# Two-layer attention block in float32 on one core: the deviation of a normalisation as a power on GpSimd, and two places in the order of the work

## The chip, the core and the metric

The kernel runs on one core of one Trainium2 chip. The metric is the device time of one execution in microseconds. One more execution was recorded by the hardware profiler; its own time stands beside its span (first to last instruction) in the table below, and every duration in this document is from such a recorded execution. Names of engines in the profile: PE is TensorE (PEld its weight loads), DVE is VectorE, ACT is ScalarE, POOL is GpSimd, SP is SyncE, which here only issues DMAs.

## The reference, cut to what matters

The input is a map of 2 x 512 channels x 64 x 32, so 2 batches of 2048 tokens with 512 channels, all in float32. Two layers follow each other:

```python
x = conv_attention(x)              # 8 heads of 64, softmax over 2048 tokens, output product, bias, + x
t = tokens(x)
t = t + landmark_attention(ln(t))  # 256 landmarks, pseudo-inverse by 6 iterations, 33-tap convolution of v
t = t + ffn(ln(t))                 # two 512 x 512 products, one of them dequantised from 4 bit
def ln(v, eps=1e-5):               # over the 512 channels
    m = mean(v, -1); s = var(v, -1)
    return (v - m) / sqrt(s + eps)
```

The change concerns the factor 1 / sqrt(s + eps) of both uses of `ln`, and the place of some steps around it and around the landmark attention.

## The kernel before, in words

Channels lie on the 128 partitions (KC = 4 chunks), tokens along the free axis in blocks of TB = 512, so a batch has NTB = 4 blocks. Heads go in pairs (NPAIR = 4). The program is written in the order in which each engine is to do its work: that order is kept on TensorE, VectorE, ScalarE and GpSimd, and units of work are interleaved by hand with Python generators. `advance(gens, n)` takes the next n units of the generators in a list and returns how many it got; where the list is empty it returns 0.

The stages, in order of time:

1. Layer 0 (to about 1420 us of the profile). `attention0` walks over pairs of a batch; each step makes scores (`sc_f`, L1072), an Exp on ScalarE (`p_f`, L1080), a running sum of exponentials on VectorE (`acc_f`, L1090) and products with the values (`av_f`, L1102). Beside it run fillers: the projections of the next pair, and, in the first pairs of batch 1, `finish0_units` for batch 0: output product and residual (`yp_f` L968, `xr_f` L975), store of x1, and the first normalisation, `norm0_steps`, which stores the normalised xh.
2. The same finish for batch 1, interleaved with the projections of layer 1 (about 1380 to 1520 us): the loop over t with `norm0(t)`, `out0(t)` and `more`, which holds the projections (`pp` L1245), landmarks (`L` L1250), and small products (`pr` L1313) of the other pairs.
3. Layer 1, pair after pair (to about 2640 us). `pinv` does the iterations of the pseudo-inverse on the matrices M and R, with `chunk(c)` and `last(i)` called between to do the attention of the pair before (`attn1_...`) and the pair after (`attn3_...`). From the fifth pair on also `finish1_units` of batch 1.
4. The last four blocks of batch 0 (to the end): output product, second normalisation, and `fp_g`, the product with the merged feed-forward matrix.

`statistics` makes the mean of a block with a product with `mean_w` (every partition then holds it, `mean_n` or `mean_g`, L990), subtracts it (`xn`, L991), squares on ScalarE (L994, L997), sums the squares on VectorE (L1002, L1003), takes their mean on TensorE (`var_n` or `var_g`, L1006), and then the square root on ScalarE with eps as bias (L1008). The result `rstd` is a tile of 128 x 512.

`norm0_steps` (layer 0's end; `rstd_n`) then takes the reciprocal on VectorE (L1023) and multiplies: half of xn on GpSimd (L1025), half on VectorE (L1026); GpSimd issues the store of xh (L1027). In batch 0 there is one xn buffer, so the next block waits for that store. `Finish1.steps` (second normalisation; `rstd_g`) takes the reciprocal on VectorE (L1660); xn stays undivided, and the factor is applied after the product: y = fp * rstd (L1683), added to the residual (L1684) and stored. Each of the two is done for 8 blocks, so there are 16 such deviations.

Exp and square root are in different activation tables on ScalarE, so loads of tables (ACT_TABLE_LOAD) stand around the square roots.

In `chunk(c)`, `attn1_sums` sums the exponentials of the pair before with ones (`rs`, L779) and copies them (L1619), `attn1_inverse` takes the reciprocal (L1624) and spreads it with eight DMAs on SP (L790), and `attn1_end`, in the next chunk, multiplies (L1631) and adds into o on GpSimd (L1632).

Of the kernel before, what the change touches and what calls it, by code (L numbers as in the profile page):

```python
# [10 lines left out]
F32 = mybir.dt.float32  # L11
I32 = mybir.dt.int32
AF = mybir.ActivationFunctionType
ALU = mybir.AluOpType
# [649 lines left out]
def fast_path(  # L664
# [96 lines left out]
    nc.vector.memset(mean_w, 1.0 / C)  # L761
    ones = const.tile([P, D], F32, name="ones1")
    nc.vector.memset(ones, 1.0)
    eps = const.tile([P, 1], F32, name="eps1")
    nc.vector.memset(eps, 1e-5)
    b0_sb = const.tile([P, KC], F32, name="b0_f")
# [26 lines left out]
    def advance(gens, n=1):  # L793


        made, i = 0, 0
        while made < n and i < len(gens):
            got = next(gens[i], gens)
            if got is gens:
                gens.pop(i)  # L800
            elif got is GAP:
                i += 1
            else:
                made += 1
        return made
# [177 lines left out]
    def statistics(xb, xn, part, name, squares, row, apart=False):  # L983


        nc.vector.tensor_tensor(part, xb[:, :2, :], xb[:, 2:, :], ALU.add)
        nc.vector.tensor_tensor(part[:, 0, :], part[:, 0, :], part[:, 1, :], ALU.add)
        yield
        mean = bank(f"mean_{name}")
        nc.tensor.matmul(mean, lhsT=mean_w, rhs=part[:, 0, :], start=True, stop=True)  # L990
        nc.vector.tensor_tensor(xn, xb, mean.unsqueeze(1).to_broadcast([P, KC, TB]), ALU.subtract)  # L991
        yield
        sq, *others = squares()
        nc.scalar.activation(sq, xn[:, :2, :], AF.Square)  # L994
        n = 2 // len(others)
        for i, other in enumerate(others):
            nc.scalar.activation(other, xn[:, 2 + i * n : 2 + (i + 1) * n, :], AF.Square)  # L997
        if apart:
            yield
        for i, other in enumerate(others):  # L1000
            to = sq[:, i * n : (i + 1) * n, :]
            nc.vector.tensor_tensor(to, to, other, ALU.add)  # L1002
        nc.vector.tensor_tensor(sq[:, 0, :], sq[:, 0, :], sq[:, 1, :], ALU.add)  # L1003
        yield
        var = bank(f"var_{name}")
        nc.tensor.matmul(var, lhsT=mean_w, rhs=sq[:, 0, :], start=True, stop=True)  # L1006
        rstd = row()
        nc.scalar.activation(rstd, var, AF.Sqrt, bias=eps, scale=1.0)  # L1008
        yield rstd

    def out0_units(b, t, xb, oTs):
# [4 lines left out]
    def norm0_steps(b, t, xb, xn, part):  # L1016

        toks = slice(t * TB, (t + 1) * TB)
        name = f"n0_{b}_{t}"
        squares = lambda: (xb[:, :2, :], xb[:, 2:, :])  # L1020
        for rstd in statistics(xb, xn, part, name, squares, lambda: deviation(name)):
            yield
        nc.vector.reciprocal(rstd, rstd)  # L1023
        wide = rstd.unsqueeze(1).to_broadcast([P, 2, TB])
        nc.gpsimd.tensor_tensor(xn[:, 2:, :], xn[:, 2:, :], wide, ALU.mult)  # L1025
        nc.vector.tensor_tensor(xn[:, :2, :], xn[:, :2, :], wide, ALU.mult)  # L1026
        nc.gpsimd.dma_start(chunked(xh_d[b])[:, :, toks], xn)  # L1027
        yield
# [605 lines left out]
    class Finish1:  # L1634
# [17 lines left out]
        def steps(self, row, apart=False):  # L1652
            def squares():
                sq = apool.tile([P, 2, TB], F32, tag="acc", name=f"sq_{self.name}")
                return sq, *(row_of(f"sq{k}_{self.name}").unsqueeze(1) for k in (2, 3))

            self.xn = self.xn()
            for rstd in statistics(self.xb, self.xn, self.xn[:, :2, :], self.name, squares, row, apart):
                if rstd is not None:
                    nc.vector.reciprocal(rstd, rstd)  # L1660
                    self.rstd = rstd
                yield

# [156 lines left out]
    for t in range(NTB):  # L1820
        more_out = [out0(t + 1)] if t + 1 < NTB else []
        advance(more)

        next(norm)
        advance(more_out or more)
        if last is not None:
            next(last)
        advance(more_out or more)
        next(norm)
        advance(more_out, 2)  # L1830
        advance(more, 2)

        next(norm)
        last = norm
        while more_out:
            advance(more_out)
        if t + 1 < NTB:
            norm = norm0(t + 1)
            next(norm)
# [90 lines left out]
    for n, pair in enumerate(todo):  # L1930
        before = todo[n - 1] if n else None
        after = todo[n + 1] if n + 1 < len(todo) else None
        if n + 2 < len(todo):
            todo[n + 2].prefetch_w()
        if n == NPAIR + 2:
            before.load_o(kvpool.tile([P, S], F32, tag="k", name=f"o2_{n - 1}"))
        if n == NPAIR + 3:

            xb = as_block(kvpool.tile([P, NST, P], F32, tag="v", name="xb_g_early"))
            xn = lambda: block_of(lpool, "xn", "xn_g_early")  # L1940
            early.append(Finish1(1, NTB - 1, [p.o for p in todo[:NPAIR]], xb, xn, True))
            before.load_o(late_buffer(f"o2_{n - 1}"))
        pair.iteration_start()
        while vals:
            advance(vals)
        if after:
            after.prefetch()
            after.attn3_begin()
        if n + 2 < len(todo):
            vals = [values(n + 2)]  # L1950
        if n:
            q = late_buffer if n > NPAIR + 1 else lambda name: kvpool.tile([P, S], F32, tag="k", name=name)
            pair.prefetch1(q(f"q2_{pair.name}"))

        def chunk(c):
            nonlocal landmarks
            if before and 0 < c <= n_ones:
                before.attn1_end(c - 1)
            if n == NPAIR and c == 1:

                finish.append(finish1_units(1, [p.o for p in todo[:NPAIR]], early))
            advance(finish)
            if c == NTB:
                if after:
                    landmarks = after.landmarks_values()
                    next(landmarks)
                    drain(convolution(n + 1))
                else:
                    advance(finish, 2)
                return  # L1970
            ones_before = before if c < n_ones else None
            if ones_before:
                if c:
                    before.attn1_scores(c, 0)
                    before.attn1_scores(c, 1)
                before.attn1_add(c)
            if after:
                for s, bank_of in ((2 * c, product_bank), (2 * c + 1, bank)):
                    after.attn3_scores(s, bank_of)
                    after.attn3_add(s)  # L1980
            else:
                advance(finish)
            if ones_before:
                before.attn1_values(c)
            if after:
                after.attn3_values(2 * c)
            else:
                advance(finish)
            if ones_before:
                before.attn1_sums(c)  # L1990
            if after:
                after.attn3_values(2 * c + 1)
            if ones_before:
                before.attn1_inverse(c)
            if n == NPAIR + 2 and c % 2:
                advance(finish)

        def last(i):
            nonlocal start
            if i == 1 and after:  # L2000
                next(landmarks)
                drain(landmarks)
                start = after.start_values()
            if i == 2 and after:
                next(start)
            else:
                advance(vals)
            if i == 3 and after:
                next(start)
            if n_ones < NTB:  # L2010

                if i == 0:
                    before.attn1_scores(n_ones, 0)
                    before.attn1_scores(n_ones, 1)
                    before.attn1_add(n_ones)
                if i == 1:
                    before.attn1_values(n_ones)
                if i == 2:
                    before.attn1_sums(n_ones)
                if i == 3:  # L2020
                    before.attn1_inverse(n_ones)
                if i == 5:
                    before.attn1_end(n_ones)
            if i == 5:
                pair.attn1_scores(0, 0)
                pair.attn1_scores(0, 1)
            advance(finish)

        landmarks = start = None
        n_ones = NTB if n + 2 < len(todo) else NTB - 1  # L2030
        pair.pinv(chunk, last)
# [158 lines left out]
```

## Time and profile before

| | |
|---|---|
| median of 2 runs | 2738.23 us (2737.63 to 2738.82) |
| the profiled execution | 2739.02 us, span 2737.2 us, TensorE clock 0.997 |
| TensorE busy | 2695.4 us (98%) |
| VectorE busy | 1631.7 us (60%) |
| ScalarE busy | 906.3 us (33%) |
| GpSimd busy | 162.0 us (6%) |

A group of instructions is given as: line, engine, operation, what it writes and reads with shapes, how many; then busy us and mean ns of one; then the idle time of the engine just before them and what ended it. A line of waits is given as: who waited for what, total us, how often, the longest. In a timeline the first number is the start in us from the span's start, the second the time that the merged entry covers, and the bracket the idle time before it and what ended it. TensorE's matmuls overlap and each float32 matmul leaves two records, so 512 columns take 0.43 us of stream time a record though one is drawn as about 0.6.

### The profile page before, as it was taken

Reading aid. Unit: us, or ns where it says so; the run is one execution under the profiler, and the core shown is the slowest. Engines: PE = TensorE matmul, PEld = TensorE weight load, DVE = VectorE, ACT = ScalarE, POOL = GpSimd, SP = SyncE. Lnnn points to the kernel's source line nnn. Section 1 sums busy time; section 2 is a strip of 40 time slices with the busy share of each in tenths; the row PEclk is TensorE's granted clock in tenths of the full one; section 3 lists DMA queues with packets and bytes.
Section 4 is the critical chain, followed back from the end, with each engine's and each line's share of the span. In section 5 each row is a group of like instructions: output and inputs, shape, how many; then the busy total and the mean of one; then the engine's idle time right before and its main releaser. Section 6 shows DMA issues by size and latency. Waiting matters only on the chain.

```text
span 2737.2 us, 41174 instructions
## 1 busy us (share of the span) xinstructions
PE 2695.4 (98%) x16994; PEld 1361.0 (50%) x16994; DVE 1631.7 (60%) x2087; ACT 906.3 (33%) x1352; POOL 162.0 (6%) x109
## 2 busy tenths in 40 slices
PE   9999999999999999999999999999999999999999
PEld 5343343434443334344344455777677666655344
DVE  3867777664557765656667544445544645465565
ACT  1434444434334334444422223223323223231210
POOL 0101011000001100000002000000000000000000
PEclk9999999999999999999999999999999999999999
DMA  4100000212111200012024632312211112111211
GB/s 147 41 11 24 24 24 24 86 36 70 32 63 57 97 24 20 24 40 77 24 89 163 209 120 93 103 34 87 81 37 62 59 44 87 44 60 53 89 39 47
DMA packets 111476, 173.99 MB, mean 64 GB/s; under 512 B 16176, under 2 KB 67888, under 8 KB 106672
## 3 DMA queue, kind: packets, MB, share of 16 engines
q1 hardware_dynamic: 105136, 150.00, 16.9%
q0 software_dynamic: 5440, 20.97, 2.1%
q8 instruction: 135, 2.21, 0.3%
q14 instruction: 61, 0.50, 0.1%
q10 hardware_dynamic: 704, 0.31, 0.0%
HBM read 90.87 MB, written 63.57 MB: 56 GB/s over the span
## 4 chain that ended last, share of the span: by engine, by line
PE 91%; DVE 5%; DMA 1%; ACT 1%; SPq 1%; issue 1%; POOL 0%; DVEq 0%; ACTq 0%; POOLq 0%
PE sc_f L1072 15%; PE av_f L1102 15%; PE pp L1245 8%; PE pa L1538 5%; PE pb L1538 5%; PE vp_f L953 4%; PE vp L953 4%; PE pp_k_f L905 4%; PE yp_g L968 4%; PE yp_f L968 4%; PE fp_g L1694 4%; PE pp_q_f L905 3%; PE av L1388 2%; PE sc L1367 2%; PE sc L1595 2%; PE av L1611 2%
## 5 line engine op out<-in xcount | busy, mean ns | idle before, releaser
L1090 DVE TENSOR_TENSOR acc_f<-acc_f,p_f 128x1024 f32<-128x1024 f32 x448 | 581.3, 1297 | 209.9 <-ACT p_f L1080 181.4
L1080 ACT ACTIVATE p_f<-sc_f 128x1024 f32<-128x1024 f32 x512 | 496.7, 1022 | 563.9 <-PE sc_f L1072 561.2
L1072 PE MATMUL sc_f<-q_f,k_f 64*64 64x512 f32 x4096 | 491.1, 594 | 2.7 <-ACT p_f L1080 2.7
L1102 PE MATMUL av_f<-p_f,v_f 64*64 64x512 f32 x4096 | 484.3, 589 | 0.0
L1102 PEld LDWEIGHTS av_f<-p_f,v_f 64*64 64x64 f32 x4096 | 156.5, 133 | 283.0 <-issue 283.0
L1072 PEld LDWEIGHTS sc_f<-q_f,k_f 64*64 64x64 f32 x4096 | 145.8, 133 | 285.6 <-issue 261.9
L1245 PE MATMUL pp<-xh,w 128*128 128x512 f32 x512 | 229.5, 600 | 0.7 <-ACT q L1248 0.7
L1538 PE MATMUL pa<-M 128*128 128x192 f32 (+1 forms) x640 | 153.1, 384 | 6.0 <-ACT M L1529 6.0
L1245 PEld LDWEIGHTS pp<-xh,w 128*128 128x128 f32 x512 | 95.3, 191 | 121.3 <-issue 113.8
L1538 PE MATMUL pb<-R 128*128 128x192 f32 (+1 forms) x640 | 149.3, 380 | 0.0
L1538 PEld LDWEIGHTS pa<-M 128*128 128x128 f32 x640 | 109.3, 195 | 27.6 <-ACT M L1529 9.1
L953 PEld LDWEIGHTS vp_f<-wv_f,x 128*128 128x128 f32 x1024 | 115.7, 192 | 13.5 <-issue 11.8
L953 PE MATMUL vp<-w,xh 128*128 128x128 f32 x1024 | 120.9, 276 | 0.0
L953 PEld LDWEIGHTS vp<-w,xh 128*128 128x128 f32 x1024 | 117.0, 192 | 7.2 <-issue 4.6
L905 PE MATMUL pp_k_f<-x,wk_f 128*128 128x512 f32 x256 | 116.0, 606 | 2.8 <-DVE k_f L908 2.4
L953 PE MATMUL vp_f<-wv_f,x 128*128 128x128 f32 x1024 | 118.7, 277 | 0.0
L1538 PEld LDWEIGHTS pb<-R 128*128 128x128 f32 x640 | 106.5, 190 | 23.2 <-DVE M L1551 0.4
L905 PE MATMUL pp_q_f<-x,wq_f 128*128 128x512 f32 x256 | 114.2, 598 | 0.8 <-DVE q_f L908 0.5
L968 PE MATMUL yp_g<-o,wo_f 128*128 128x512 f32 x256 | 114.8, 597 | 0.0
L968 PE MATMUL yp_f<-q_f,wo_f 128*128 128x512 f32 x256 | 113.5, 598 | 0.8 <-DVE xr_f L975 0.8
L1120 POOL TENSOR_TENSOR q_f<-q_f,rinv_f 128x512 f32<-128x512 f32 x32 | 46.7, 1459 | 1039.3 <-DMA rinv_f<-acc_f 761.1
L1551 DVE SCALAR_TENSOR_TENSOR R<-M,pa 128x320 f32<-128x320 f32 (+1 forms) x160 | 59.9, 416 | 67.8 <-PE pa L1538 67.8
(210 smaller groups left out, 2764.8 us busy)
## 6 DMA issues: line engine op xcount, KB each, us to landing
xh<-xh_fd SPq DMA_DIRECT2D x12, 1024.0 KB, 5.5
rinv_f<-acc_f SPq DMA_DIRECT2D x256, 32.0 KB, 1.9
xr_f<-in_x_dram SPq DMA_DIRECT2D x8, 1024.0 KB, 5.2
x_fd<-xr_f POOLq DMA_DIRECT2D x8, 1024.0 KB, 4.8
xh_fd<-xn_f POOLq DMA_DIRECT2D x8, 1024.0 KB, 4.7
k_fd<-k SPq DMA_DIRECT2D x32, 256.0 KB, 2.9
q_fd<-q SPq DMA_DIRECT2D x32, 256.0 KB, 2.9
k<-k_fd SPq DMA_DIRECT2D x8, 1024.0 KB, 6.6
```

The lines of the kernel that those rows point to most:

```text
L905: nc.tensor.matmul(pp, lhsT=w_sb[kind][:, k, cols], rhs=xbs[t][:, k, :], start=k == 0, stop=k == KC - 1)
L953: nc.tensor.matmul(vp[:, j * P : (j + 1) * P], lhsT=xb[:, k, j * P : (j + 1) * P], rhs=w_of(k), start=k == 0, stop=k == KC - 1,)
L968: nc.tensor.matmul(yp, lhsT=wo_sb[:, k, m * P : (m + 1) * P], rhs=oTs[k][:, toks], start=k == 0, stop=k == NPAIR - 1,)
L1072: nc.tensor.matmul(sc[r * D : (r + 1) * D, h, :], lhsT=hd.k[rows, lo : lo + D], rhs=hd.q[rows, t * TB : (t + 1) * TB], start=True, stop=True,)
L1080: nc.scalar.activation(p, sc, AF.Exp, scale=D**-0.5)
L1090: nc.vector.tensor_tensor(acc, first if c == 1 else acc, p, ALU.add)
L1102: nc.tensor.matmul(av[r][half, :], lhsT=hd.v[keys, c, half], rhs=pp[keys, h, :], start=c == 0, stop=c == NST - 1,)
L1245: nc.tensor.matmul(pp, lhsT=self.w[j][:, c, :], rhs=xhs[t][:, c, :], start=c == 0, stop=c == KC - 1)
L1367: nc.tensor.matmul(scs[h][:, j * LM : (j + 1) * LM], lhsT=self.k[rows, c * P : (c + 1) * P], rhs=self.L[0][rows, :], start=True, stop=True,)
L1538: nc.tensor.matmul(dst, lhsT=lhsT[:, k, t * P : (t + 1) * P], rhs=rhs[:, k, :], start=k == 0, stop=k == 1)
L1551: nc.vector.scalar_tensor_tensor(out, m, scale, pr, ALU.mult, ALU.subtract)
L1694: nc.tensor.matmul(fp[:, cols], lhsT=mT[:, k, m * P : (m + 1) * P], rhs=self.xn[:, k, cols], start=k == 0, stop=k == KC - 1,)
```

## The change

The square root becomes an Identity (variance plus eps, out of the accumulator), and GpSimd takes it to the power -0.5 in place, with a constant tile of one column spread over the row. The two reciprocals on VectorE go, and so do 19 of the 20 table loads that lie on the executed path. Two places of the order change. In the loop of stage 2, where no output units are left (the last block), four units of `more` instead of two come between the squares and the variance. In `chunk(c)`, the sums `attn1_sums` come after the second half of `attn3_values` instead of before it.

```diff
@@ constants
     nc.vector.memset(ones, 1.0)
+    power = const.tile([P, 1], F32, name="power1")
+    nc.vector.memset(power, -0.5)
@@ statistics
         nc.tensor.matmul(var, lhsT=mean_w, rhs=sq[:, 0, :], start=True, stop=True)
         rstd = row()
-        nc.scalar.activation(rstd, var, AF.Sqrt, bias=eps, scale=1.0)
+        nc.scalar.activation(rstd, var, AF.Identity, bias=eps, scale=1.0)
+        nc.gpsimd.tensor_tensor(rstd, rstd, power.to_broadcast([P, TB]), ALU.pow)
         yield rstd
@@ norm0_steps
-        nc.vector.reciprocal(rstd, rstd)
         wide = rstd.unsqueeze(1).to_broadcast([P, 2, TB])
         nc.gpsimd.tensor_tensor(xn[:, 2:, :], xn[:, 2:, :], wide, ALU.mult)
         nc.vector.tensor_tensor(xn[:, :2, :], xn[:, :2, :], wide, ALU.mult)
@@ Finish1.steps
                 if rstd is not None:
-                    nc.vector.reciprocal(rstd, rstd)
                     self.rstd = rstd
                 yield
@@ the loop of stage 2
         advance(more_out or more)
         next(norm)
-        advance(more_out, 2)
-        advance(more, 2)
+        advance(more, 2 if advance(more_out, 2) else 4)
 
         next(norm)
@@ chunk(c)
-            if ones_before:
-                before.attn1_sums(c)
             if after:
                 after.attn3_values(2 * c + 1)
             if ones_before:
+                before.attn1_sums(c)
                 before.attn1_inverse(c)
```

In the built order of the engines this moves `var_n` of the last block of batch 1 behind four more `pp` matmuls and two `pr`; it moves `rs` behind four `av` matmuls in 23 chunks; GpSimd gets 16 instructions, each ahead of the product or the addition that follows; VectorE loses 16.

## The prediction

> **What bounds the kernel now.** I read the page's busy times and chain first, then the list of waits by engine, the groups of instructions by shape, and the timeline wherever a statistic of the two normalisations is made. From the page:
>
> ```profile
> PE 2695.4 (98%) x16994; PEld 1361.0 (50%) x16994; DVE 1631.7 (60%) x2087; ACT 906.3 (33%) x1352; POOL 162.0 (6%) x109
> PE 91%; DVE 5%; DMA 1%; ACT 1%; SPq 1%; issue 1%; POOL 0%; DVEq 0%; ACTq 0%; POOLq 0%
> ```
>
> TensorE is the bound: of 2737.2 us it is idle for 41.8. The change takes no matmul away, so it can earn only from those 41.8 us and from matmuls that run slow after an idle stretch. VectorE has time on average, but an in-order VectorE that stands still in the wrong place stops TensorE. The waits of TensorE say where (total, times, longest):
>
> ```profile
> PE pa L1538 <- ACT M L1529: 6.0, 2, 4.6
> PE var_n L1006 <- issue: 3.7, 1, 3.7
> PE wp L1513 <- DVE R L1551: 3.2, 2, 2.1
> PE p_pa L1528 <- DVE M L1502: 2.2, 2, 1.2
> PE mean_n L990 <- DVE xn_f L987: 1.4, 1, 1.4
> PE yp_f L968 <- DVE xr_f L975: 0.8, 1, 0.8
> ```
>
> The work that the change replaces, in groups by shape (busy us, mean ns), with GpSimd's nearest instruction last:
>
> ```profile
> L1023 DVE RECIPROCAL rstd_n<-rstd_n 128x512 f32<-128x512 f32 x8 | 26.7, 3342 | 0.0
> L1660 DVE RECIPROCAL rstd_g<-rstd_g 128x512 f32<-128x512 f32 x8 | 26.8, 3352 | 15.3 <-ACT rstd_g L1008 15.3
> L1008 ACT ACT_TABLE_LOAD x10 | 12.8, 1283 | 7.1 <-PE var_n L1006 7.0
> L1120 POOL TENSOR_TENSOR q_f<-q_f,rinv_f 128x512 f32<-128x512 f32 x32 | 46.7, 1459 | 1039.3 <-DMA rinv_f<-acc_f 761.1 <-DVE acc_f L1090 278.2
> ```
>
> The largest stall that belongs to the change, in the timeline (start, us):
>
> ```profile
> 1486.96 3.34 DVE L1023 RECIPROCAL rstd_n<-rstd_n 128x512 f32<-128x512 f32 x1
> 1489.62 3.70 PE L1245 MATMUL pp<-xh,w 128*128 128x512 f32 x8
> 1494.96 1.21 DVE L1002 TENSOR_TENSOR xr_f<-xr_f 128x1024 f32<-128x1024 f32 x1
> 1496.21 0.69 DVE L1003 TENSOR_TENSOR xr_f<-xr_f 128x512 f32<-128x512 f32 x1
> 1497.00 1.48 PE L1006 MATMUL var_n<-xr_f,mean_w 128*128 128x512 f32 x2 [3.68 <-issue]
> 1498.28 4.95 PE L1245 MATMUL pp<-xh,w 128*128 128x512 f32 x8
> ```
>
> TensorE stands until VectorE ends L1003 at 1496.90. VectorE has no gap there: its reciprocal of the block before (1486.96) is in front. After the stall eight matmul records take 4.95 us where they took 3.70.
>
> **What the Trainium skill says.** "ScalarE: Activation LUTs", What ACT_TABLE_LOAD costs: about 1283 ns for a load and 1380 ns of drain for every switch of set; the same page, Table sets, says identity is filler in every set. The trace agrees on 1283 and shows no drain: the load at 2541.11 starts 0.02 us after the instruction before it. "GPSIMD Engine Reference", Elementwise: bodies of three and more operations go at about 3 a cycle, a two-input add at 2.6 cycles an element. The trace agrees with the second (undisturbed 128x512 products take 1.27 us); neither page nor trace prices a power. "TensorE: Matmul & The Clock Gate", Part 1, has an idle array fall to half clock; the 4.95 against 3.70 above agrees.
>
> **The change part by part.**
>
> *Removed from VectorE:* 16 reciprocals x 3.35 = 53.5 us. *From ScalarE:* 19 of 20 table loads x 1.283 = 24.4 us; the Identity that replaces Sqrt keeps its 0.69. Both are off the path except where a wait above hangs on them:
> - 1497.00: 3.68 idle, + 1.25 slow matmuls, + 0.46 of the longer var = 5.4 us. Twice cured: VectorE is 3.3 us earlier, and the new filler count puts var behind four more pp matmuls and two pr. Next late would be pr, which needs X; VectorE makes X_0 by about 1495, and TensorE reaches pr at about 1496.8.
> - 2449.02: wp waits 1.19 for R, which stands behind the reciprocal L1660 (2445.38 to 2448.73). Gone. The inverse of the row sums behind it starts 4 us earlier, so the DMA for which VectorE idles until 2458.54 lands earlier; that clears 1.00 us at 2461.53.
> - 912.24 (0.82) and 920.80 (1.43): the residual add, and the reuse of the one xn buffer after GpSimd's product and its store, follow the reciprocal of 906.92.
> - 936.26 (0.73): scores wait for an Exp behind the table load at 933.89.
> Sum 10.6 us. The other waits for ScalarE and VectorE (4.6 at 2527, 2.1 at 2440, 1.5 at 2596) have neither a reciprocal nor a load ahead of them and stay.
>
> *Added to GpSimd:* 16 powers of 128x512. Not in the trace. Below: not under a product of the same shape, 1.3 us. Above: a power is a logarithm, a product and an exponential; as polynomials with exponent handling I count 20 to 40 operations for each of 512 elements. At the page's 3 per cycle (1.2 GHz) that is an estimate of 3 to 6 us; if nothing overlaps, at some 4 cycles each, 34 to 68 us. I take **7 us**, near the geometric middle of 1.3 and 40.
>
> It is hidden as long as it ends before its first reader comes up. The room, from the end of Sqrt (less a table load just before it) to that reader's start: batch 0: 17.9, 10.5, 8.4, 7.1 us; batch 1: 11.8, 11.4, 12.5, about 8; first finish: 36.8, 6.6, 4.9, 3.8; last four blocks: 3.9 (the power starts at 2647.9 behind GpSimd's last o add, its reader came at 2651.80), 19.5, 19.5, 3.3. In the finish and the last blocks the reader, y, has 3 to 5 us more, since fp banks stand ready: in the last block VectorE idles 2.0 us twice before 2731.07, so 8.9 us are free; in the block at 2647.9, 6.4, until the squares of the next block are late for var at 2657.89. With 7 us only this one shows: 0.6. Behind a waiting VectorE stand the exponential sums (batch 0), the landmark means and squares (batch 1), R and M of the inverse (finish); TensorE waits for these. GpSimd itself has only o products and x1, xh stores behind it, read much later except for the xn reuse named above.
>
> *Moved:* in 23 chunks rs goes behind the second four av matmuls. The three parts take 0.96 + 0.57 + 1.02 us at 1853.52; sixteen av records in one go take 1.95 at 1763.40, so 0.02 us x 23 = 0.5 is won. But rs, its copy, its reciprocal and the eight spread DMAs on SP start 1 us later. Mostly covered (VectorE idles 0.8 us after that reciprocal at 1857.34), but not at 2515.45, where R follows it at once, nor at 2522.34, where VectorE already waits for that DMA ahead of the 4.6 us stall. I take 1.5 lost: net +1.0 (bounds -0.5 and +3).
>
> Sum: -10.6 + 0.6 + 1.0 = **-9.0 us**. The profiled execution took 2739.0 (span 2737.2 and 1.8 around it), 0.8 over the median, so 2730 against it and **2729** against the median of 2738.2.
>
> **The rivals.**
> 1. *The power is partly exposed* (8 to 18 us). For it: three rooms are under 5 us and no row bounds the power. At 13 us the overruns of all sites add to 64, less some 20 of bank reserve; if half of the rest reaches TensorE, 22 lost against 9 won: about 2752.
> 2. *The power is slow, and VectorE stalls in order behind it* (slower). Place: L1026 and L1683 on VectorE. Price: at 25 us the overruns add to 226, less 20; seven tenths reach TensorE (there is no other work once buffers are full): 144 - 10 gives about 2870. It decides from about 18 us, where the loss passes 54. Against it: GpSimd is 6% busy and its product runs near its price.
> 3. *The cleared waits come back behind others.* GpSimd and VectorE slow each other (products reach 2.3 us beside VectorE work against 1.27), or pr waits for X: half of the gain stays, about 2735.
>
> **How the numbers follow.** Main case 0.54, rival 1 0.20, rival 2 0.16, rival 3 0.10. Two per cent, 55 us, is about what a measurement of this kernel can tell from no change; a gain of that size is more than all 41.8 us of idle time, so faster gets 0.01. Slower is rival 2, 0.16; the rest, 0.83, is within. The range runs from 2722 (power under 4 us, more waits cleared than counted) to 2775 (power of 16 us): the main case, rival 3 and most of rival 1.
>
> **What would show it.** Right: no L1023 and L1660, one table load, powers of 128x512 on GpSimd near 7 us, no idle time before var_n at 1497 and before wp at 2449, TensorE idle near 32 us. Wrong: VectorE idle before L1026 or L1683 released by GpSimd, with TensorE waiting for acc, xn or R just after; a power over 18 us turns the sign beyond doubt. If the power is under 8 us and the time still does not fall, rival 3 holds.

## The result, and the profile after

The changed kernel took 3854.77 us (median of 2 runs, 3854.45 to 3855.09) against 2738.23: a ratio of 1.408 [1.405, 1.410]. It is slower by 1116 us, where the prediction had 2729 and a range of 2722 to 2775. Line numbers of the changed kernel are one to three higher than those of the kernel before. A site is one of the 16 normalisations; the room of a power is the time from its start until its reader is ready for it. Its profiled execution took 3854.45 us, span 3853.0.

From its page: TensorE's busy time, the granted clock in 40 slices, and the chain that ended last.

```profile
PE 2727.2 (71%) x16994; PEld 1377.2 (36%) x16994; DVE 1577.2 (41%) x2072; ACT 880.0 (23%) x1333; POOL 1472.8 (38%) x125
...
PEclk9999999978766999996665999999997968757665
...
PE 56%; POOL 34%; DVE 4%; issue 2%; DMA 1%; SPq 1%; ACT 1%; DVEq 0%; POOLq 0%; ACTq 0%
```

GpSimd rose from 162 us to 1473 and now holds a third of the chain, where it held nothing. TensorE's work is the same 16994 records; its idle time rose from 41.8 to 1125.8, and its busy time by 31.8. These two, 1084.0 and 31.8, are the whole growth of the span, 1115.8. The clock row (tenths of full clock) has its low digits in the stretches of the normalisations and 9s between them.

The two groups of powers (line, engine, operation, shapes, count; busy us, mean ns of one; idle before and what ended it):

```profile
L1011 POOL TENSOR_TENSOR rstd_n<-rstd_n,power 128x512 f32<-128x512 f32 x8 | 655.8, 81976 | 103.8 <-ACT rstd_n L1010 103.8
...
L1011 POOL TENSOR_TENSOR rstd_g<-rstd_g,power 128x512 f32<-128x512 f32 x8 | 655.9, 81984 | 77.8 <-ACT rstd_g L1010 77.8
```

One power of 128x512 takes 82.0 us, not 7. Its readers on VectorE, from the list of waits (who waited for what: total us, times, longest):

```profile
DVE xn_f L1028 <- POOL rstd_n L1011: 598.1, 8, 80.3
DVE y_g L1684 <- POOL rstd_g L1011: 569.0, 8, 81.4
```

All 16 readers stand still, 1167.1 us together, nine tenths of the 1311.7 us of powers. The largest waits of TensorE do not name GpSimd; it waits for what VectorE, or ScalarE beside it, would have done next:

```profile
PE yp_f L970 <- DVE xr_f L977: 337.0, 5, 74.5
PE var_g L1008 <- DVE sq_g L1005: 189.7, 4, 75.2
PE sc L1597 <- DVE y_g L1684: 150.3, 2, 75.4
PE sc_f L1074 <- ACT p_f L1082: 77.5, 9, 75.2
PE tp L1524 <- DVE y_g L1684: 73.2, 1, 73.2
PE pr L1315 <- DVE X L1301: 73.0, 1, 73.0
```

Each longest wait here is one power less 7 to 9 us. The row var_n at 1497, the largest stall that the change was to clear, is gone. One site in the timeline (start, us, then idle time and what ended it in the bracket), the first of batch 0:

```profile
783.72 81.94 POOL L1011 TENSOR_TENSOR rstd_n<-rstd_n,power 128x512 f32<-128x512 f32 x1 [2.35 <-ACT rstd_n L1010]
...
804.46 3.70 PE L970 MATMUL yp_f<-q_f,wo_f 128*128 128x512 f32 x8
808.09 1.95 PE L1074 MATMUL sc_f<-q_f,k_f 64*64 64x512 f32 x16
809.25 1.94 ACT L1082 ACTIVATE p_f<-sc_f 128x1024 f32<-128x1024 f32 x2 [5.29 <-PE sc_f L1074]
809.86 1.90 PE L1104 MATMUL av_f<-p_f,v_f 64*64 64x512 f32 x16
865.70 1.22 DVE L1028 TENSOR_TENSOR xn_f<-xn_f,rstd_n 128x1024 f32<-128x1024 f32 x1 [67.40 <-POOL rstd_n L1011]
866.84 0.74 DVE L977 SCALAR_TENSOR_TENSOR xr_f<-yp_f,b_f,xr_f 128x512 f32<-128x512 f32 x1
867.64 5.39 PE L970 MATMUL yp_f<-q_f,wo_f 128*128 128x512 f32 x8 [55.88 <-DVE xr_f L977]
```

The chain reads from bottom to top. TensorE stands 55.88 us for a bank (a block of the accumulator) that L977 on VectorE must empty; L977 is behind L1028 in VectorE's fixed order; L1028 waits for the power. VectorE stopped at 798.3; TensorE had other work up to 811.8, and then nothing. Eight output-product records right after the stall take 5.39 us; the same eight took 3.70 just before it. While TensorE has nothing to do here, from 812 to 865 us, the granted clock is 0.54 of full. Such slow stretches after a stall make up the additional busy time: the group yp_f alone grew from 113.5 us to 126.1.

### The profile page after: what moved, and what is told of

Read it like the earlier page. It is cut to its first block, busy times and chain, and to the rows that moved or that the text cites. A ratio compares the mean times of both kernels' runs of the same rounds, so it can differ in the third digit from the quotient of the medians.

```text
span 3853.0 us, 41154 instructions
## 1 busy us (share of the span) xinstructions
PE 2727.2 (71%) x16994; PEld 1377.2 (36%) x16994; DVE 1577.2 (41%) x2072; ACT 880.0 (23%) x1333; POOL 1472.8 (38%) x125
## 4 chain that ended last, share of the span: by engine, by line
PE 56%; POOL 34%; DVE 4%; issue 2%; DMA 1%; SPq 1%; ACT 1%; DVEq 0%; POOLq 0%; ACTq 0%
POOL rstd_n L1011 17%; POOL rstd_g L1011 17%; PE sc_f L1074 10%; PE av_f L1104 9%; PE pp L1247 5%; PE pb L1540 3%; PE pa L1540 3%; PE vp L955 3%; PE vp_f L955 3%; PE pp_k_f L907 3%; PE pp_q_f L907 2%; PE yp_g L970 2%; PE yp_f L970 2%; PE sc L1597 2%; DVE acc_f L1092 1%
## 5 line engine op out<-in xcount | busy, mean ns | idle before, releaser
L1011 POOL TENSOR_TENSOR rstd_n<-rstd_n,power 128x512 f32<-128x512 f32 x8 | 655.8, 81976 | 103.8 <-ACT rstd_n L1010 103.8
L1011 POOL TENSOR_TENSOR rstd_g<-rstd_g,power 128x512 f32<-128x512 f32 x8 | 655.9, 81984 | 77.8 <-ACT rstd_g L1010 77.8
L970 PE MATMUL yp_f<-q_f,wo_f 128*128 128x512 f32 x256 | 126.1, 649 | 337.0 <-DVE xr_f L977 337.0
L1634 POOL TENSOR_TENSOR o<-o,rinv 128x512 f32<-128x512 f32 x32 | 44.6, 1395 | 705.3 <-DVE rinv L1633 636.2
L1684 DVE TENSOR_TENSOR y_g<-fp_g,rstd_g 128x512 f32<-128x512 f32 (+1 forms) x33 | 22.0, 666 | 580.2 <-POOL rstd_g L1011 569.0
L1028 DVE TENSOR_TENSOR xn_f<-xn_f,rstd_n 128x1024 f32<-128x1024 f32 x8 | 9.8, 1225 | 598.1 <-POOL rstd_n L1011 598.1
L970 PEld LDWEIGHTS yp_f<-q_f,wo_f 128*128 128x128 f32 x256 | 51.7, 208 | 410.2 <-DVE xr_f L977 341.2
L1597 PE MATMUL sc<-q,L 64*128 64x512 f32 x224 | 62.2, 644 | 151.0 <-DVE y_g L1684 150.3
L1008 PE MATMUL var_g<-sq_g,mean_w 128*128 128x512 f32 x16 | 11.6, 813 | 189.7 <-DVE sq_g L1005 189.7
L1602 ACT ACTIVATE p<-sc 128x512 f32<-128x512 f32 x128 | 66.7, 601 | 250.8 <-PE sc L1597 250.5
```

Source lines behind the costliest of these rows:

```text
L970: nc.tensor.matmul(yp, lhsT=wo_sb[:, k, m * P : (m + 1) * P], rhs=oTs[k][:, toks], start=k == 0, stop=k == NPAIR - 1,)
L1011: nc.gpsimd.tensor_tensor(rstd, rstd, power.to_broadcast([P, TB]), ALU.pow)
L1597: nc.tensor.matmul(sc, lhsT=self.Lk[rows, j * P : (j + 1) * P], rhs=self.q[rows, t * TB : (t + 1) * TB], start=True, stop=True,)
L1602: nc.scalar.activation(p[:, h, :], sc, AF.Exp, scale=D**-0.5)
```

## The experiments

Four questions were open. What does a power cost, and on what does it depend? Does the sum of the prediction hold if the power has the size that was assumed? How much of VectorE's waiting reaches TensorE? And what are the other parts of the change worth without the power?

### The price of a power by itself: e5_price

```diff
 (kernel before, at its start, on constant tiles)
+for p, n in ((P, 512), (P, 128), (P, 32), (P, 4), (1, 128), (16, 128), (32, 128)):
+    nc.gpsimd.tensor_tensor(made[:p, :n], base[:p, :n], power[:p].to_broadcast([p, n]), ALU.pow)
+nc.gpsimd.tensor_tensor(made[:, :128], base[:, :128], power.to_broadcast([P, 128]), ALU.mult)
```

> The kernel before with eight GpSimd instructions on constant tiles at its start: powers of 128x512, 128x128, 128x32, 128x4, 1x128, 16x128 and 32x128 (base 0.7, exponent -0.5) and one product of 128x128. If a power goes column by column[...], time follows the columns alone: 82, 20.5, 5.1, 0.7, and 20.5 us for 1, 16 and 32 partitions. If it goes value by value,[...] 1x128 takes a sixteenth of 16x128, about 1.3 us, while 16, 32 and 128 partitions still take 20.5.

Measured, groups by shape on GpSimd:

```profile
L770 POOL TENSOR_TENSOR bench_out<-bench_in,power 128x512 f32<-128x512 f32 x1 | 82.0, 81982 | 1.3 <-DVE bench_in L767 1.3
L770 POOL TENSOR_TENSOR bench_out<-bench_in,power 128x128 f32<-128x128 f32 x1 | 20.7, 20720 | 0.1
L770 POOL TENSOR_TENSOR bench_out<-bench_in,power 1x128 f32<-1x128 f32 x1 | 20.7, 20715 | 0.1
L770 POOL TENSOR_TENSOR bench_out<-bench_in,power 16x128 f32<-16x128 f32 x1 | 20.7, 20705 | 0.1
L770 POOL TENSOR_TENSOR bench_out<-bench_in,power 128x32 f32<-128x32 f32 x1 | 5.4, 5416 | 0.1
L770 POOL TENSOR_TENSOR bench_out<-bench_in,power 128x4 f32<-128x4 f32 x1 | 1.0, 1006 | 0.1
L771 POOL TENSOR_TENSOR bench_out<-bench_in,power 128x128 f32<-128x128 f32 x1 | 0.4, 399 | 0.1
```

Only the number of columns counts: (81.98 - 20.72) / 384 = 0.160 us a column, and some 0.3 us besides. One partition costs as much as 128. The 82 us of the changed kernel is thus the operation itself: at the start of the program, on other data and beside other work, it is the same to 0.01 us. The product of 128x128 (last line) with the same spread operand takes 0.40 us, so it is the power and not the form of the instruction. The whole kernel took 2845.95 us in its one run, with 172 us of these instructions in front; that time is not used.

### The change with a power of 44, 80, 128 and no columns: e2_pow44, e9_pow80, e3_pow128, e4_nopow

```diff
 (changed kernel; n = 44, 80 or 128. The other columns keep variance plus eps)
-nc.gpsimd.tensor_tensor(rstd, rstd, power.to_broadcast([P, TB]), ALU.pow)
+some = rstd[:, :n]
+nc.gpsimd.tensor_tensor(some, some, power.to_broadcast([P, n]), ALU.pow)
 (e4_nopow: the line is left out altogether)
```

44 columns:

> The changed kernel with the power taken of the first 44 of 512 columns, so that it should last about 7 us (82 us x 44/512), the size that the prediction assumed; the other columns keep variance + eps. Theory (the mechanism was right and only the size of one power wrong): the prediction's sum holds, about 2729. Rival (a power on GpSimd costs more than its time, through the shared interface or the queue behind it): above 2740.

80 columns:

> The power of the first 80 columns only (the rest of 1 / sigma is left as the variance); at 160 ns a column some 13.1 us each, the size at which the prediction's first rival was priced. The prediction's own conversion (the overruns of all sites add to 64 us, less 20 of bank reserve, half reaches TensorE, 9 won elsewhere) gives 2752. The rival reading, after the run of 128 columns: nearly every microsecond that VectorE waits reaches TensorE, and more; between the runs of 44 columns (41.7 us of VectorE waits, no loss) and 128 (207 us of waits, 157 us lost) that puts the waits near 105 us and the time near 2790.

128 columns:

> The changed kernel with the power taken of the first 128 of 512 columns, about 20.5 us each; the other columns keep variance + eps. Theory (TensorE loses the overrun of each power over its room, the part that the buffers take left off): the rooms listed in the prediction are overrun by 158 us in all, less 20 of reserve, two thirds of it lost: 2800 to 2840. Rival (what counts is whether a power is there, not how long): near 3855, or near 2729.

None:

> The changed kernel without the power: Identity alone gives the factor, so the root and its inverse are left out. It is what the change saves, with nothing in return. Theory: the five waits that hang on table loads and reciprocals go, 10.6 us, less 1 for the moved row sums: about 2729. Rival (cleared waits come back behind others): 2733 or more, at the level of the moves alone.

VectorE's waits for the power, for 44, 80 and 128 columns in this order:

```profile
DVE y_g L1685 <- POOL rstd_g L1012: 29.4, 5, 7.7
DVE xn_f L1029 <- POOL rstd_n L1012: 12.3, 4, 5.7
```
```profile
DVE y_g L1685 <- POOL rstd_g L1012: 58.0, 5, 13.4
DVE xn_f L1029 <- POOL rstd_n L1012: 50.6, 7, 12.0
```
```profile
DVE xn_f L1029 <- POOL rstd_n L1012: 109.6, 8, 19.6
DVE y_g L1685 <- POOL rstd_g L1012: 97.8, 6, 21.0
```

With the times beside them:

| columns | one power, us | VectorE waits for it, us | time, us | ratio to before |
|---|---|---|---|---|
| none | - | - | 2726.08 | 0.9955 [0.9939, 0.9972] |
| 44 | 7.47 | 41.7 | 2730.92 | 0.9973 [0.9962, 0.9985] |
| 80 | 13.19 | 108.6 | 2805.73 | 1.0251 [1.0235, 1.0267] |
| 128 | 20.78 | 207.4 | 2894.36 | 1.0569 [1.0552, 1.0587] |
| 512 | 81.98 | 1167.1 | 3854.77 | 1.4077 [1.4054, 1.4099] |

First, at the size that the prediction assumed, the whole change takes 2730.9, against 2729 predicted: the sum comes out, in part by luck, since VectorE waits 41.7 us where an overrun of 0.6 was booked, and the gains split otherwise than forecast (below). Second, the first 42 us of VectorE's waiting cost about 5 us (4.8; the two intervals overlap), and from there on a microsecond of waiting is about a microsecond of time. Between the rows the waits grow by 66.9, 98.8 and 959.7 and the time by 74.8, 88.6 and 960.4: 1.1, 0.9 and 1.0. Both the run of 80 columns (expected 2752 by the prediction's own conversion, 2790 by the other reading) and the run of 128 (2800 to 2840) came out above what was expected. At 80 columns the waits were as expected (105) and more of them reached the time; at 128 the overruns were put too low as well, 158 us where VectorE waits 207.4. Counted from the kernel without a power, the waits cost 4.8, 79.7, 168.3 and 1128.7 us, so 37, 29, 39 and 38 us of them are absorbed: a reserve of about 2 us a site, whatever the length of the power. It is used up once; behind it everything counts. Third, if the time grows evenly between 44 and 80 columns, the change is level with the kernel before at a power of about 8 us and loses 2% (2793 us) at about 12; no run lies between.

### Is it VectorE's wait, or GpSimd's being busy? e10_unread

```diff
 (changed kernel; readers of rstd find variance plus eps, without root and inverse)
-nc.gpsimd.tensor_tensor(rstd, rstd, power.to_broadcast([P, TB]), ALU.pow)
+for lo in range(0, TB, 64):
+    nc.gpsimd.tensor_tensor(unread, rstd[:, lo : lo + 64], power.to_broadcast([P, 64]), ALU.pow)
```

> The changed kernel, but each power of 512 columns is taken in eight pieces of 64 into a small tile that nobody reads, so that GpSimd is as busy as before (about 84 us a site) and the readers of 1 / sigma find plain variance plus eps without waiting (the root and the inverse are left out of what they read). If the loss comes from VectorE standing in order before the scaling of y and x-hat, the 569 us of the two finish stages and the last blocks go, and the row y from 1 / sigma behind GpSimd is near zero; what is left is batch 0 and 1, where GpSimd's own half of the x-hat scaling stands behind the power and the one buffer of xn, or the one row of sigma, comes free late: 3000 to 3400. If GpSimd merely being busy costs the time (a shared port, its queue), the time stays near 3850. If only VectorE's wait counts, it falls to about 2730.

Measured: 3699.84, a ratio of 1.352 [1.350, 1.354]: 155 us less than the changed kernel and outside the 3000 to 3400 that I expected. The rows of VectorE waiting for the power are gone, as they must be. In their place (some rows of the list of waits of all engines):

```profile
ACT xr_f L997 <- DMA x_fd<-xr_f: 250.2, 3, 86.4
DVE xr_f L1005 <- ACT xr_f L1000: 239.6, 4, 80.4
...
DVE xn_f L989 <- DMA xh_fd<-xn_f: 190.1, 3, 78.3
...
DVE y_g L1686 <- POOL o L1636: 135.3, 2, 74.0
ACT rstd_g L1011 <- POOL unread L1013: 120.6, 2, 69.4
```

And the last entry of GpSimd's timeline:

```profile
3352.38 339.24 POOL L1013 TENSOR_TENSOR unread<-rstd_g,power 128x64 f32<-128x64 f32 x32
```

The first of these rows stands in the changed kernel too (L996 there: 241.3 us, 3 times, longest 83.4) and not in the list of the kernel before. The stores of x1 and xh, the o products and the one row of rstd all stand behind the power in GpSimd's order or are held by it, and each now stops VectorE or ScalarE for most of a power. The end was not reckoned in my expectation: the powers of the last four blocks run back to back to 3691.6 us, while VectorE's last instruction ends at 3528.4, so some 163 us of the span are powers whose result nobody reads. Even without them the time would be near 3530 (an estimate), above my range and 800 us above the kernel without a power. Neither simple theory holds. A power of 82 us holds this program up in two ways that overlap in the changed kernel: through its reader, and through all that is queued behind it on GpSimd. Removing only the first leaves most of the loss; how the loss of the changed kernel splits between the two is not shown. That a busy GpSimd slows VectorE's instructions themselves is not seen: VectorE's busy time for the same 2072 instructions is 1577.2 us in the changed kernel and 1577.7 in e4_nopow, without any power.

### The parts without the power: e1_orders, e6_filler, e7_swap

```diff
 (kernel before, square root and reciprocals as they were)
 e1_orders: both hunks; e6_filler: only the first; e7_swap: only the second
-        advance(more_out, 2)
-        advance(more, 2)
+        advance(more, 2 if advance(more_out, 2) else 4)
@@ chunk(c)
-            if ones_before:
-                before.attn1_sums(c)
             if after:
                 after.attn3_values(2 * c + 1)
             if ones_before:
+                before.attn1_sums(c)
                 before.attn1_inverse(c)
```

Both:

> The kernel before with only the two moves of the change (four units of filler ahead of the last variance of batch 1, the row sums after the second half of the values); square root and reciprocal stay. Theory (the slowdown is the power alone): within 5 us of before, about 2735, since the filler clears a stall of 3.7 to 5.4 us and the moved row sums cost about 1. Rival (the new order is part of the loss): clearly above 2745.

The filler count:

> The kernel before with only the filler count changed (four units of other work ahead of the last variance of batch 1). Theory: the stall of 3.7 us before var at 1497 and the half clock after it go, 3.5 to 5.4 us faster: 2733 to 2735. Rival (pr, next in line, waits as long for X): no difference.

The row sums:

> The kernel before with only the row sums moved behind the second half of the values in 23 chunks. By the prediction's working it loses about 1 us (0.5 won in transitions, up to 3 lost where the row sums and their DMA come later): 2738 to 2741. If TensorE's changes of tile shape cost more than I read, it wins: 2730 to 2736.

Measured: both 2731.27, 0.9974 [0.9963, 0.9984]; the filler count alone 2736.14, 0.9993 [0.9986, 0.9999]; the row sums alone 2735.01, 0.9989 [0.9982, 0.9996]. With the filler count the wait of 3.68 for var_n is gone, but two waits of TensorE that the kernel before did not show stand in its list:

```profile
PE pr L1313 <- DVE X L1299: 1.8, 1, 1.8
PE pr L1313 <- ACT rstd_n L1008: 1.2, 1, 1.2
```

So 3.0 of the 3.7 us came back behind pr, which was moved ahead of var: with the reciprocals still in VectorE's order, X is late. What is left of the gain is the slow stretch after the stall: the group pp is busy for 227.7 us in place of 229.5, var_n for 8.7 in place of 9.0.

The move of the row sums won about 3 us, where I had expected it to cost 1. The trace shows where. One chunk in the kernel before, and the same in e7_swap (TensorE alone; between the lines stand rs and, before, the second half of av):

```profile
1853.52 1.03 PE L1388 MATMUL av<-p,v 128*64 128x256 f32 x8
...
1856.07 0.33 PE L1528 MATMUL p_pa<-ident,M 128*128 128x128 f32 x1
```
```profile
1850.38 1.90 PE L1388 MATMUL av<-p,v 128*64 128x256 f32 x16
...
1852.78 0.33 PE L1528 MATMUL p_pa<-ident,M 128*128 128x128 f32 x1
```

The same 24 records take 2.55 us before and 2.40 after, in each of the 23 chunks: 0.15 x 23 = 3.5 us, near the 3.0 that the medians differ by.

### The inverse and the root: e11_no_inverse, e8_lnexp, e12_ln_exp_orders

```diff
 e11_no_inverse (both moves of order, square root kept; 1 / sigma stays sigma)
-        nc.vector.reciprocal(rstd, rstd)          (both places)
 e8_lnexp (the filler count) and e12_ln_exp_orders (both moves), reciprocals taken out
-        nc.scalar.activation(rstd, var, AF.Sqrt, bias=eps, scale=1.0)
+        nc.scalar.activation(rstd, var, AF.Ln, bias=eps, scale=1.0)
+        nc.scalar.activation(rstd, rstd, AF.Exp, scale=-0.5)
```

> The kernel before with both moves of order and the square root kept, but without the 16 reciprocals (1 / sigma stays sigma: the inverse is left out). It splits the 5 us between the run of the two moves alone (2731.3) and the run with Identity alone (2726.1) into reciprocals and table loads. The prediction gives the reciprocals the waits at 2449, 2461, 912 and 920, 4.4 us, and the table loads 0.7: about 2727. The rival, that the loads in front of the scores and the Square cost as much: about 2729.5.

> The kernel before with the filler count of the change, and 1 / sigma as exp(-0.5 ln(variance + eps)) in two ScalarE instructions in place of square root and reciprocal; GpSimd gets nothing. VectorE is rid of its 16 reciprocals, ScalarE gets 16 more instructions of 0.7 us and 32 table loads stand where 19 stood. If VectorE's reciprocals are what the waits hang on: near the kernel without any power, about 2728. If the table loads are: no better than the filler alone or worse, 2733 to 2740.

> A complete kernel that takes the root and the inverse off both VectorE and GpSimd: exp(-ln(var + eps) / 2) on ScalarE, with both moves of order. 32 table loads of 1.28 us where the kernel before has 20 of them on ScalarE. With the filler count alone this gave 2735.9, no more than the filler count without it (2736.1). If the moves add, 2731, no better than the moves alone; if the reciprocals' going is worth more than twelve loads cost, below 2730, and this is the best version.

Measured: without the inverse 2730.27, 0.9972 [0.9962, 0.9982], the same as the moves alone (0.9974); logarithm and exponential with the filler count 2735.86, 0.9992 [0.9983, 1.0001], and with both moves 2732.72, 0.9980 [0.9974, 0.9987]. Without the reciprocals the four waits of TensorE that the prediction hung on them are gone (wp, for instance, is down from 3.2 to 2.1), and so is that of 1.8 for X; but a wait of mean_n for part_f, 0.4 in the kernel before, has grown to 4.0 (TensorE's list of e11_no_inverse):

```profile
PE mean_n L990 <- DVE part_f L987: 4.0, 2, 2.4
...
PE wp L1512 <- DVE R L1550: 2.1, 1, 2.1
PE pr L1312 <- ACT rstd_n L1008: 1.2, 1, 1.2
```

Why part_f comes late is not shown. Loads do stand in the way at one place: in e12_ln_exp_orders the scores wait 2.52 us at 932.63, behind two loads and the additional activation, where the kernel before has 0.73 at 936.26. But neither reciprocals nor table loads, taken singly, are worth anything that these runs can tell once the order is changed: what their going clears is given back by another wait, or lies within what the runs resolve. I had the reciprocals at 4.4 us here. Leaving out reciprocals and table loads together (e4_nopow, 0.9955) is the lowest time of all, but its interval overlaps that of the moves alone, so how 5 us split between them stays open. The best complete version found is the two moves alone, 7 us or 0.26% below the kernel before; taking the inverse off VectorE through ScalarE does not add to it.

## Why the prediction was wrong, point by point

**The step that failed: "I take 7 us", with "Above: ... 20 to 40 operations".** The term measured 81.98 us, twelve times the value taken and twice the upper bound of 40 that was kept for the range. It was reckoned from a count of operations at the rate that the Trainium skill gives in "GPSIMD Engine Reference", Elementwise, for bodies of three and more. The measurement decides: 82 us for 512 columns, whatever the number of partitions. At the 1.2 GHz that the prediction used, 0.160 us is an estimate of 192 cycles a column, against 7 to 13 at the page's rate and 80 to 160 if nothing overlaps. The prediction's 34 to 68 for operations that don't overlap was nearer, though its upper end was too low as well; yet it was cut to 40 and then averaged with 1.3, the price of a product. A power is no small multiple of a product: a product grows by 2.3 ns a column (0.40 us at 128 columns, 1.27 at 512), a power by 160. That difference is also what supports the page's 2.6 cycles for a two-input operation (2.7 here, as an estimate at 1.2 GHz); the 1.27 us alone, which the prediction set beside it, is 3.0 cycles a column. No row of the trace of before priced the power; the listed rooms are 20 us or less at all sites but one, and most of the interval from 1.3 to 68 lies above that (on the geometric scale that was used, still a third of it), so the 0.16 for a slow power was too small by the prediction's own numbers.

**The rooms were right in their order of size, but too large.** Power less the reader's wait gives the room in the profile after. First finish: 81.98 - 46.40 = 35.6, listed 36.8. Batch 0: 14.5, 7.1, 5.0, 3.7, against 17.9, 10.5, 8.4, 7.1 listed. Each of the four is 3.4 too large: I counted up to the reader's start in the kernel before, and the reciprocal of 3.35 that stood right before it (799.31, reader at 802.69) goes with the change, so that the reader comes up that much earlier. The other short rooms shrank too: the last of batch 1, listed as about 8, was 1.7; in the finish 1.5, 0.9 and 3.3 stood for 6.6, 4.9 and 3.8. Together this is why powers of 7.47 us already make VectorE wait 41.7 us, where the overruns of the list as it stood add to 15.

**What that wait costs.** "In the finish ... 3 to 5 us more, since fp banks stand ready" holds for TensorE, though not for VectorE, which stops all the same. Against the kernel without a power (e4_nopow: TensorE busy 2686.7 of 2723.6 us), TensorE loses 1089 of the 1167 us of VectorE's waits as idle time and some 40 as slow matmuls after it, so 38 us, 2.4 a site, are absorbed. "Half of the rest" at 13 us and "seven tenths" at 25 were too low; past the reserve all of it counts. With 82 us in place of 7, the listed rooms (186 us in sum) leave 1312 - 186 = 1126 us, which is the loss against the kernel without a power (1128.7) to 1%. That is luck in part, since two slips cancel: the rooms were 41 us too large, and 38 us were absorbed.

**The mechanism that came was the second rival's**, at the place it named (VectorE in order at the two readers, now L1028 and L1684), by the price it could not know. Its threshold of 18 us was late: a power of 13.2 us already makes the kernel 2.5% slower. "A power over 18 us turns the sign beyond doubt" was true.

**"GpSimd itself has only o products and x1, xh stores behind it, read much later"** is wrong at this size, as the powers that nobody reads show: stores and o products behind an 82 us instruction keep buffers from coming free, and so stop VectorE and ScalarE. At 7 us it does not show in the time.

**The gains and the moves.** Everything but the power gave -11.9 us (e4_nopow) where the working has -10.6 + 1.0. The total is about right, in part by luck, for the split is not. The filler count alone gave 1.9 (0.0007 of 2738), not the 5.4 booked for it with the earlier reciprocal, because pr came up late (the third rival's second mechanism, on a small scale; the prediction had X in time, but with the reciprocals gone). The move of the row sums was booked at +1.0 with bounds of -0.5 and +3; it gave about -3. The term that failed there is 0.02 us a chunk, which measured 0.15: it was read from the sixteen av records at 1763.40, which take 1.95 us and come shortly after a stall of TensorE, while sixteen in the moved place take 1.82. The loss of 1.5 on the DMAs did not show. The waits named for the reciprocals did go, as e11_no_inverse shows, but 3.6 us came back at mean_n, which is the third rival's case; what is left of them is below what the runs resolve.

## What to carry to other kernels

An operation that no row of the trace shows has no price: one such instruction by itself at the start of the kernel gives it, as e5_price did here. Without that, compare the slowest reading (here 68 us, and even that was too low) with the room, and where the room lies inside the bounds put the chance there, not at the middle. Count the room to the point where the reader is ready in the new order, with what was removed in front of it taken out. An instruction that is longer than the slack of an in-order engine's next reader cost nearly its whole excess once for each use here, and taking the reader away did not help much while stores and other work stood behind it in its own engine's queue.

## What the runs showed of the hardware

A float32 power on GpSimd costs 0.160 us a column and the same for 1, 16, 32 or 128 partitions: 82 us for 512 columns, where a product of 128x512 takes 1.27. After long stalls TensorE starts slow: eight records took 5.39 us against 3.70, after a stretch without matmuls in which the granted clock was 0.54, and over the whole program this made some 40 us of busy time more than in the kernel without a power. That is in accord with "TensorE: Matmul & The Clock Gate", Part 1, of the Trainium skill, which has an idle array fall to half clock.
